# Local attention layers of a two-branch network: scores and value sums in 64x32 tiles of TensorE, values in fp32 kept in SBUF, another step order

## The chip, the cores and the metric

The kernel runs on one core of one Trainium2 chip. The metric is the device time of one execution in microseconds (us), the median over the runs. Engines are named as in the profile: PE (TensorE matmuls), PEld (its weight loads), DVE (VectorE), ACT (ScalarE), POOL (GpSimd), SP (SyncE, which issues all DMAs here).

## The reference

The input x is 2048 tokens of 128 numbers. It is normalised to xn, and two branches work on xn: a global low-rank attention of 16 heads, and a stack of six local layers. The result is x + global(xn) + local(xn). The change is in the local layers only. Cut to what matters, one of them is:

```python
def attn_layer(x, Wqkv, qs, ksc, Wo):            # x: tokens shifted by one in half of the channels
    q, k, v = split(x @ Wqkv)                    # 16 heads of 64, 128 -> 3 * 1024
    q, k = l2norm(q) * qs, l2norm(k) * ksc
    q, k = rotary(q), rotary(k)                  # with a scale per position
    # windows of 32 tokens; each sees its own and the one before: 64 keys
    sim = einsum('bhwie,bhwje->bhwij', bq, bk2) * 8.0      # masked to 32 back
    out = einsum('bhwij,bhwje->bhwie', softmax(sim), bv2)
    return out @ Wo                              # 1024 -> 128
def ffn_layer(x, g, bln, W1, b1, W2, b2):        # layernorm, 128 -> 2 * 341, a * gelu(gate), -> 128
for i in range(6):
    x = attn_layer(shift_tokens(x), ...) + x
    x = ffn_layer(shift_tokens(x), ...) + x
```

All inputs and outputs are fp32.

## The kernel before, in words

The program has two stages on the same core. The global attention comes first, with the loading of the first local weights woven in; then `LocalStack.run` does the six local layers. This stage goes over 48 steps, one for each layer L and each slice s of 256 tokens (8 slices a layer). A step consists of some 120 small pieces, each a method of `LocalStack`: `q`, `k`, `v` (projections, g from 0 to 3 for groups of four heads), `S` (scores), `sa` (mask added, out of PSUM), `mx`, `sub`, `Pr`, `ex`, `su` (softmax), `pp` and `PT` (transpose of the weights, and its eviction), `av` (value sums), `O` (divided by the sums, out of PSUM), `ot`, `oh`, `wo` (output projection), `xb` to `ffo` (feed-forward). The text `ORDER` lists all pieces with a lag, as `S.3@3`. Round n of `run` goes through this list once and does each piece for step n minus its lag, so that pieces of several steps alternate; the instructions are issued on each engine exactly in that order, and nothing reorders them (`manual_schedule`). There are 48 rounds plus the largest lag, 6.

Projections are done in split precision: the input is rounded to `xhead` with rest `xtail`, the weights to `wh` with rest `wl`, both in fp32r, and three products are added (`xh`, `xl`, `w_head`, `w_tail`; L597 for q and k, L673 for v).

Scores: a tile `kbd` of keys is block diagonal. Its 128 partitions are two heads of 64; where one head has its keys, the other has zeros. `S` (L818) does for each window of 32 tokens and each pair of heads one matmul with 128 contracted rows, 32 columns of weights (the queries) and 128 moved columns (64 keys of each of two heads), 16 for each g. They go to four 32-partition strips of one PSUM bank.

Values: `v` projects a group of heads for 256 tokens, `vc` evicts it into `vn`, `vd` stores it in DRAM, and `lv` loads it back as overlapping windows of 64 tokens into block-diagonal tiles `vbd`; `av` (L876) then does 16 matmuls of 128 rows, 32 columns of weights and 128 moved columns for each g.

PSUM has eight banks here: three of pool `pj` (projections; slots handed out by `take` and given back by `done`), two of `pT` (transposes), one for `S`, one for `av` (`pS`, `pO`), and one accumulator of `wo`.

Of the kernel before, what the change touches and what calls it, by code (L numbers as in the profile page):

```python
# [11 lines left out]
ALU = mybir.AluOpType  # L12
# [49 lines left out]
class GlobalAttention:  # L62
# [334 lines left out]
    k.0@1 wh.w1@6 ex.0@3 q1.3@2 k.1@1 tabq@1 oh.1@4 rb@2 wd.qkv.3@2 nl@5 q.0@1 O.3@4 wh.qkv.2@2 qa.0@2 lv.0.1@3 k1.0@1  # L397
    ks.1@1 sub.1@3 k2.0@1 wo.0@4 fd@6 pp.0@3 k2.1@1 wh.qkv.0@1 qa.1@2 ks.0@1 wt.w1@6 PT.0@3 ot.2@4 su.0@3 v.3@2 Pr.1@3
    qs.0@1 sa.2@3 vc.3@2 qr.1@2 k1.1@1 oh.2@4 wo.1@4 wt.qkv.2@2 ot.3@4 wd.qkv.1@1 gate@5 q1.0@1 ex.1@3 q2.0@1 wo.2@4
    oh.3@4 pp.1@3 wt.qkv.0@1 km.0@2 wh.qkv.3@2 q.2@1 mx.2@3 su.1@3 wo.3@4 fe@6 ff@6 S.3@3 xb@4 sa.3@3 av.0@3 km.1@2  # L400
    gelu@5 ka.0@1 qs.2@1 mean@4 PT.1@3 q1.2@1 v.1@1 xc@4 q2.2@1 xh@0 sub.2@3 wt.qkv.3@2 vc.1@1 O.0@3 mx.3@3 lv.1.1@3
    l0@5 km.2@2 k.2@1 vd.1@2 k.3@1 av.1@3 Pr.2@3 m0@5 ka.1@1 ww.w2@6 ks.2@1 ks.3@1 ex.2@3 k2.2@1 ha.0@1 x2@4 selk@1
    k2.3@1 kb.0@2 pp.2@3 km.3@2 qa.3@2 ot.0@3 O.1@3 sk@1 wd.qkv.0@0 k1.2@1 q.1@1 wd.w1@5 oh.0@3 k1.3@1 qs.1@1 q.3@1
    q2.1@1 ww.wo.1@4 ww.wo.0@4 qs.3@1 xl@0 qa.2@2 S.0@2 selq@1 wh.qkv.1@1 PT.2@3 var@4 q1.1@1 su.2@3 sq@1 ha.1@1
    sa.0@2 l1@5 ptn@1 sn@1 v.2@1 sub.3@3 vd.0@1 ka.3@1 Pr.3@3 lv.1.0@3 ln@4 rs@1 av.2@3 mx.0@2 wt.qkv.1@1 vc.2@1
    kb.1@2 rn@1 ex.3@3 S.1@2 ptk@1 nw@4 tabk@0 rk@1 pp.3@3 m1@5 sub.0@2 fa@5 PT.3@3 xr@4 q2.3@1 fb@5 aff@4 v.0@0 w2@5
    tk@0 O.2@3 Pr.0@2 fc@5 av.3@3 su.3@3 qr.0@1 rd@1 sa.1@2 wd.qkv.2@1 S.2@2 mx.1@2 lv.0.0@2 ot.1@3 ffo@5 vc.0@0
    ka.2@1
# [3 lines left out]
class LocalStack:  # L412
# [15 lines left out]
    def __init__(self, tc, ctx, io, const, xa, yd, out):  # L428
        self.tc, self.nc, self.io, self.c = tc, tc.nc, io, const
        self.xa, self.yd, self.out = xa, yd, out  # L430
        self.wl = {}
        self.pj = self.pT = None
        self.st = {}
        self.pw = ctx.enter_context(tc.tile_pool(name="b_w", bufs=1))
        self.pr = ctx.enter_context(tc.tile_pool(name="b_raw", bufs=1))
        self.pe = ctx.enter_context(tc.tile_pool(name="b_early", bufs=1, reuse_waits="tile"))
        self.free = {"raw": [0, 1], "pj": [0, 1, 2], "pt": [0, 1]}
        self.users = {}

    def take(self, kind, key, shape, users):  # L440

        pool = {"raw": self.pr, "pj": self.pj, "pt": self.pT}[kind]
# [16 lines left out]
    def w_whole(self, key, tag, src):  # L459
        w = self.wl[key] = self.pw.tile(list(src.shape), F32, tag=tag, name="w")  # L460
        self.nc.sync.dma_start(out=w, in_=src)
# [20 lines left out]
    def w_src(self, L, kind, i):  # L482
# [3 lines left out]
            "w1": lambda: io["w1"][L], "w2": lambda: io["w2"][L],  # L486
        }[kind]()

    def first_weights(self):
        self.vectors(0)  # L490
        for kind, i in (("wo", 0), ("wo", 1), ("w2", 0)):
# [37 lines left out]
    def buffers(self, ctx):  # L529
        nc = self.nc  # L530

# [6 lines left out]
        self.pS = pool("b_s", space=PSUM)  # L538
        self.pO = pool("b_o", space=PSUM)
# [3 lines left out]
        self.kbd = [self.pb.tile([128, 2, 2, 2, TS + 32], F32, name=f"kbd{i}") for i in range(2)]  # L543
        self.vbd = [self.pb.tile([128, 4, 2, 256], F32, name=f"vbd{i}") for i in range(3)]
        self.vn = [self.pb.tile([128, 4, 2, 2, 64], F32, name=f"vn{i}") for i in range(2)]
        for t in self.kbd:
            for j in range(2):
                nc.vector.memset(t[64 * j : 64 * j + 64, :, :, 1 - j, :], 0.0)
        for t in self.vbd:
            for j in range(2):  # L550
                nc.gpsimd.memset(t[64 * j : 64 * j + 64, :, 1 - j, :], 0.0)
        self.vturn = 0
# [114 lines left out]
    def v(self, L, s, g):  # L667
        xh, xl = self.st["xhead", L, s], self.st["xtail", L, s]
        wh, wl = self.wl["qkv", L, g]
        ps = self.take("pj", ("ps_v", L, s, g), [128, 2, 256], 1)  # L670
        for t in range(2):
            for i, (a, b) in enumerate(((xh, wh), (xh, wl), (xl, wh))):
                self.nc.tensor.matmul(ps[:, t, :], a[:, bass.ts(t, 128)], b[:, 512:768], start=(i == 0), stop=(i == 2))  # L673

    def vc(self, L, s, g):
        key = ("ps_v", L, s, g)
        self.nc.scalar.copy(
            self.vn[g // 2][:, :, g % 2], self.st[key].rearrange("p t (j q e) -> p (t j) q e", j=2, q=2)
        )
        self.done(key)  # L680

    def vd(self, L, s, gg):
        nc = self.nc
        if s == 0:
            self.st["vd", L, gg] = self.pd.tile([T + 32, 512], F32, tag=f"vd{gg}", name=f"vd{gg}_{L}")
            nc.sync.dma_start(
                out=self.st["vd", L, gg][0:32, :].rearrange("t (a e) -> t a e", a=2), in_=self.vbd[0][64:96, 0:2, 0, :]
            )
        nc.sync.dma_start(
            out=self.st["vd", L, gg][32 + s * TS : 32 + (s + 1) * TS, :].rearrange("(t p) e -> p t e", p=128),  # L690
            in_=self.vn[gg].rearrange("p (t j) g q e -> p t (j g q e)", t=2),
        )

    def lv(self, L, s, gg, i):

        vd, vbd = self.st["vd", L, gg], self.vbd[self.vturn % 3]
        self.vturn += 1
        self.st["vbd", L, s, gg, i] = vbd
        t0 = s * TS + 128 * i
        for j in range(2):  # L700
            src = vd[t0 : t0 + 64, 256 * j : 256 * j + 256]
            src = bass.AP(src.tensor, src.offset, [[512, 64], [32 * 512, 4], [1, 256]])
            self.nc.sync.dma_start(out=vbd[64 * j : 64 * j + 64, :, j, :], in_=src)
# [96 lines left out]
    def kb(self, L, s, gg):  # L800
        keys = self.st["keys", L, s, gg]
        for p in range(2):
            for j in range(2):
                for half in range(2):
                    lo, src = 64 * j + 32 * half, 32 * (2 * p + j)
                    self.nc.sync.dma_start(  # L806
                        out=self.kbd[gg][lo : lo + 32, :, p, j, :], in_=keys[src : src + 32, :, half, :]
# [3 lines left out]
    def S(self, L, s, g):  # L811
        kbd, q = self.kbd[g // 2][:, g % 2], self.st["t1q", L, s, g]
        S = self.st["S", L, s, g] = self.pS.tile([128, 8, 64], F32, tag="S", name="S")
        for i in range(2):
            for p in range(2):
                for w in range(4):
                    W = 4 * i + w
                    self.nc.tensor.matmul(  # L818
                        S[32 * w : 32 * w + 32, 4 * i + 2 * p : 4 * i + 2 * p + 2, :],
                        q[:, p, 32 * W : 32 * W + 32],  # L820
                        kbd[:, p, :, 32 * W : 32 * W + 64],
                        start=True, stop=True,
                    )

    def sa(self, L, s, g):
        S, P, mask = self.st["S", L, s, g], self.tile(("P", L, s, g), [128, 8, 64], 2), self.c["mask"]
        for i in range(2):
            if s == 0 or i == 0:
                h = slice(4 * i, 4 * i + 4 if s == 0 else 8)
                m = bmid(mask[:, i if s == 0 else 1, :], h.stop - h.start)  # L830
                self.nc.vector.tensor_tensor(P[:, h, :], S[:, h, :], m, ALU.add)
# [429 lines left out]
```

## Time and profile before

| | |
|---|---|
| median of 3 runs | 2295.75 us (2295.43 to 2300.25) |
| the profiled execution, its own time | 2285.88 us |
| its span, first to last instruction | 2284.0 us |
| mean granted PE clock in it | 0.987 of full |
| instructions | 69814, of them 27556 PE matmuls and as many weight loads |
| DMA packets, bytes | 295074, 382.40 MB |

A line of the profile for a group of instructions gives line, engine and operation, result<-operands, shapes (partitions x elements; for a matmul rows\*columns of the array, then partitions x moved columns), the count, busy time and the mean of one. An fp32 matmul stands in the trace as two records, one for each pass; an fp32r matmul as one. In a line of the stretches, each engine's busy time has its count of instructions behind it; then come the granted PE clock, the DMA engines' share and GB/s. In a line of the order of time, start and length come first; the length of a matmul has its pipeline in it, so that the start of the next block tells what one costs.

### The profile page before, as it was taken

Reading aid. Unit: us, or ns where it says so; the run is one execution under the profiler, and the core shown is the slowest. Engines: PE = TensorE matmul, PEld = TensorE weight load, DVE = VectorE, ACT = ScalarE, POOL = GpSimd, SP = SyncE. Lnnn points to the kernel's source line nnn. Section 1 sums busy time; section 2 is a strip of 40 time slices with the busy share of each in tenths; the row PEclk is TensorE's granted clock in tenths of the full one; section 3 lists DMA queues with packets and bytes.
Section 4 is the critical chain, followed back from the end, with each engine's and each line's share of the span. In section 5 each row is a group of like instructions: output and inputs, shape, how many; then the busy total and the mean of one; then the engine's idle time right before and its main releaser. Section 6 shows DMA issues by size and latency. Waiting matters only on the chain.

```text
span 2284.0 us, 69814 instructions
## 1 busy us (share of the span) xinstructions
PE 2191.6 (96%) x27556; PEld 1612.5 (71%) x27556; DVE 1880.7 (82%) x2981; ACT 1755.8 (77%) x3389; POOL 1395.3 (61%) x1417
## 2 busy tenths in 40 slices
PE   8999999999997899999999999999999999998987
PEld 3444444444445788888888888888888888887765
DVE  7999999999985687888888888788888888887764
ACT  6999999999985576777777777777777777776654
POOL 4000100000006887988898889888898888888662
PEclk9999999999999999999999999999999999999998
DMA  3223232222214788878888878888888888787662
GB/s 106 54 66 81 60 73 65 56 60 57 64 37 145 210 219 212 226 222 231 217 237 218 225 218 225 229 233 222 219 224 225 224 225 230 216 228 202 180 188 71
DMA packets 295074, 382.40 MB, mean 167 GB/s; under 512 B 38300, under 2 KB 228508, under 8 KB 293276
## 3 DMA queue, kind: packets, MB, share of 16 engines
q1 hardware_dynamic: 294732, 377.92, 61.7%
q8 instruction: 220, 3.60, 0.7%
q14 instruction: 106, 0.87, 0.1%
q10 hardware_dynamic: 16, 0.00, 0.0%
HBM read 195.06 MB, written 75.50 MB: 118 GB/s over the span
## 4 chain that ended last, share of the span: by engine, by line
PE 76%; DMA 7%; POOL 5%; SPq 4%; DVE 3%; ACT 3%; issue 2%; POOLq 0%; DVEq 0%; ACTq 0%
PE y L285 11%; PE st L275 9%; PE s L251 7%; PE ps_wo L904 5%; PE ps_o L876 5%; PE S L818 5%; PE ps_q L597 5%; PE ps_k L597 5%; PE ps_v L673 3%; PE pt_p L854 3%; PE ps_n L710 3%; PE pt_o L892 3%; SPq L806 2%; PE ps_w L1019 2%; PE ps_h L972 2%
## 5 line engine op out<-in xcount | busy, mean ns | idle before, releaser
L254 DVE TENSOR_REDUCE m<-s 128x1 f32<-128x1024 f32 x512 | 602.8, 1219 | 31.1 <-PE s L251 20.9
L277 ACT ACTIVATE p<-st 128x512 f32<-128x512 f32 x1024 | 542.4, 598 | 41.1 <-PE st L275 11.0
L305 POOL TENSOR_TENSOR z<-z 72x512 f32<-72x512 f32 x15 | 19.2, 1279 | 559.3 <-DMA z<-yp 559.3
L285 PE MATMUL y<-p,zv 128*9 128x256 f32 x4096 | 293.1, 381 | 2.3 <-ACT ysb L295 2.3
L798 POOL TENSOR_TENSOR keys<-keys,rbt 128x512 f32<-128x512 f32 x192 | 244.7, 1285 | 78.4 <-DMA rbt<-rd 75.8
L251 PE MATMUL s<-ks,qs 64*128 64x512 f32 x1024 | 280.9, 447 | 1.7 <-ACT ks L156 1.7
L275 PE MATMUL st<-qs,ks 64*128 64x512 f32 x1024 | 272.8, 433 | 1.0 <-ACT p L277 0.8
L654 POOL TENSOR_TENSOR t1q<-t1q,ur 128x512 f32<-128x512 f32 x192 | 246.7, 1286 | 24.9 <-DMA ur<-t2q 16.5
L624 POOL TENSOR_TENSOR keys<-keys,t2k 128x512 f32<-128x512 f32 x192 | 246.7, 1285 | 11.8 <-DVE keys L613 5.7
L876 PE MATMUL ps_o<-vbd,PTt 128*32 128x128 f32 x6144 | 209.0, 277 | 9.0 <-DMA vbd<-vd 7.4
L275 PEld LDWEIGHTS st<-qs,ks 64*128 64x128 f32 x1024 | 139.7, 184 | 108.1 <-ACT p L277 88.8
L818 PE MATMUL S<-kbd,t1q 128*32 128x128 f32 x6144 | 212.4, 280 | 3.0 <-DMA kbd<-keys 3.0
L838 POOL TENSOR_TENSOR P<-P,m 128x512 f32<-128x512 f32 x192 | 200.6, 1045 | 11.9 <-DVE m L834 7.3
L842 POOL TENSOR_TENSOR P<-P,r 128x512 f32<-128x512 f32 x192 | 200.6, 1045 | 0.5
L904 PE MATMUL ps_wo<-OT,w 128*128 128x256 f32 x768 | 197.1, 379 | 0.0
L876 PEld LDWEIGHTS ps_o<-vbd,PTt 128*32 128x32 f32 x6144 | 161.6, 110 | 38.4 <-ACT nh L959 13.9
L251 PEld LDWEIGHTS s<-ks,qs 64*128 64x128 f32 x1024 | 120.8, 185 | 95.0 <-issue 86.0
L818 PEld LDWEIGHTS S<-kbd,t1q 128*32 128x32 f32 x6144 | 169.0, 112 | 25.7 <-issue 16.9
L628 DVE SCALAR_TENSOR_TENSOR t1q<-ps_q,vec,tabq 128x512 f32<-128x512 f32 x192 | 143.2, 746 | 48.1 <-PE S L818 25.2
L285 PEld LDWEIGHTS y<-p,zv 128*9 128x9 f32 x4096 | 74.4, 89 | 149.0 <-issue 96.2
L658 ACT ACTIVATE sq<-ps_k 128x512 f32<-128x512 f32 x192 | 114.3, 598 | 82.6 <-PE ps_k L597 74.3
L638 DVE SCALAR_TENSOR_TENSOR t2q<-ps_q,vec,tabq 128x512 f32<-128x512 f32 x192 | 142.5, 742 | 40.5 <-ACT sq L658 38.8
(204 smaller groups left out, 5743.5 us busy)
## 6 DMA issues: line engine op xcount, KB each, us to landing
vbd<-vd SPq DMA_DIRECT2D x384, 256.0 KB
kbd<-keys SPq DMA_DIRECT2D x768, 72.0 KB
vd<-vn SPq DMA_DIRECT2D x96, 512.0 KB
ur<-t2q SPq DMA_DIRECT2D x384, 128.0 KB
rbt<-rd SPq DMA_DIRECT2D x192, 128.0 KB
tabk<-in_rope SPq DMA_DIRECT2D x48, 384.0 KB
yp<-ysb SPq DMA_DIRECT2D x64, 256.0 KB
tabq<-in_rope SPq DMA_DIRECT2D x48, 256.0 KB
```

The lines of the kernel that those rows point to most:

```text
L251: nc.tensor.matmul(s[:, j, :], q[:, bass.ts(qt, 128)], k[:, bass.ts(2 * hf + j, 512)], start=True, stop=True)
L254: nc.vector.tensor_reduce(self.mrow[h, qt // 4][:, qt % 4, hf : hf + 1], s.rearrange("p a b -> p (a b)"), AX.X, ALU.max)
L275: nc.tensor.matmul(st, k[:, bass.ts(kb, 128)], q[:, bass.ts(qb, 512)], start=True, stop=True)
L277: nc.scalar.activation(p, st, AF.Exp, scale=float(1.0 / 8.0**0.5))
L285: self.nc.tensor.matmul(self.y[32 * c : 32 * c + 9, cols], self.zv[:, kb, h, :], self.pts[h, qb, kb][:, cols], start=(j == 0 and half == 0 ...
L597: self.nc.tensor.matmul(ps[:, p, :], a[:, c], b, start=(i == 0), stop=(i == 2))
L624: self.nc.gpsimd.tensor_tensor(t, t, self.st["t2k", L, s, g], ALU.add)
L654: self.nc.gpsimd.tensor_tensor(t, t, self.st["ur", L, s, g // 2][:, g % 2], ALU.add)
L798: self.nc.gpsimd.tensor_tensor(t, t, bmid(self.st["rbt", L, s][:, g, :], 2), ALU.mult)
L818: self.nc.tensor.matmul(S[32 * w : 32 * w + 32, 4 * i + 2 * p : 4 * i + 2 * p + 2, :], q[:, p, 32 * W : 32 * W + 32], kbd[:, p, :, 32 * W ...
L876: self.nc.tensor.matmul(ps[32 * w : 32 * w + 32, i, p, :, :], PT[:, i, p, 32 * w : 32 * w + 32], vbd[:, w, :, c : c + 64], start=True, sto ...
L904: self.nc.tensor.matmul(self.st["acc", L, s], w[:, 2 * (g % 2) + c, :], o[:, c, :], start=(g == 0 and c == 0), stop=(g == 3 and c == 1),)
```

## The change

- Scores: `kbd` has no zeros and holds each head's keys in its own 64 partitions. `S` does a matmul for each head: 64 rows, 32 columns of weights, 64 moved columns; 32 for each g instead of 16. The two heads of a pair write to two banks.
- Value sums: `av` likewise, 32 matmuls of 64 rows and 32 columns, 64 moved columns.
- Values: `v` multiplies 64 tokens of the unsplit input `xa` by unsplit fp32 weights `wv` for all 16 heads, in two matmuls of 64 weight columns and 512 moved columns; `vc` evicts them to the odd windows of `vw`; `vx` builds the even (overlapping) windows with copies between partitions of SBUF by DMA. `vn`, `vd`, `lv` and `vbd` go, and the values' DRAM round trip with them; the split weights `wqkv` shrink from 768 to 512 columns a group.
- PSUM: `S` and `av` share one slot of two banks ("so"), taken by the one or the other, and given back by `sa` and by `O`.
- The list `ORDER` is another one; the largest lag is 4. Its start, and the places around `S` and `av`:

```
    av.2@3 wt.qkv.1@1 sub.0@2 q2.2@1 q1.3@1 v.0@1 O.2@3 q2.3@1 v.1@1 xh@0 rs@1 tabk@0 wd.qkv.2@1 rn@1 Pr.0@2 kb.1@2
    ...
    ks.2@0 k.3@0 su.3@2 wo.0@2 ks.3@0 selk@0 S.0@1 ww.wo.1@3 wh.qkv.0@0 PT.2@2 sk@0 k2.2@0 q.2@0 k2.3@0 PT.3@2 x2@3
    k1.2@0 ha.1@0 q.3@0 qa.2@1 qa.3@1 sa.0@1 qs.2@0 wt.qkv.0@0 qs.3@0 wd.qkv.1@0 ot.1@2 k1.3@0 S.1@1 vx@1 wh.qkv.1@0
    ka.2@0 su.2@2 selq@0 q1.2@0 mx.0@1 oh.1@2 var@3 sq@0 ptn@0 sa.1@1 sn@0
```

On PE the eight blocks of a round then stand so: av.2, v.0, v.1, av.3, v.2, (k), v.3, S.3, (wo, gate), av.0, (l0), S.2, (wo, l1, q, w2), av.1, (k, mean, wo, norm sums), S.0, (q, ot), S.1, (norm sums, variance).

```diff
-        self.free = {"raw": [0, 1], "pj": [0, 1, 2], "pt": [0, 1]}
+        self.free = {"raw": [0, 1], "pj": [0, 1, 2], "pt": [0, 1], "so": [0]}
...
-        self.kbd = [self.pb.tile([128, 2, 2, 2, TS + 32], F32, name=f"kbd{i}") for i in range(2)]
-        self.vbd = [self.pb.tile([128, 4, 2, 256], F32, name=f"vbd{i}") for i in range(3)]
-        self.vn = [self.pb.tile([128, 4, 2, 2, 64], F32, name=f"vn{i}") for i in range(2)]
+        self.kbd = [self.pb.tile([128, 2, 2, TS + 32], F32, name=f"kbd{i}") for i in range(2)]
...
-        ps = self.take("pj", ("ps_v", L, s, g), [128, 2, 256], 1)
-        for t in range(2):
-            for i, (a, b) in enumerate(((xh, wh), (xh, wl), (xl, wh))):
-                self.nc.tensor.matmul(ps[:, t, :], a[:, bass.ts(t, 128)], b[:, 512:768], start=(i == 0), stop=(i == 2))
+        ps = self.take("pj", ("ps_v", L, s, w), [128, 512], 1)
+        t0 = s * TS + 64 * w
+        for j in range(2):
+            self.nc.tensor.matmul(ps[64 * j : 64 * j + 64, :], self.xa[:, t0 : t0 + 64], wv[:, j, :], start=True, stop=True)
...
+    def vx(self, L, s):
+        nc, vw = self.nc, self.st["vw", L, s]
+        for j in range(2):
+            a, z = slice(64 * j, 64 * j + 32), slice(64 * j + 32, 64 * j + 64)
+            nc.sync.dma_start(out=vw[z, 0:8:2, :], in_=vw[a, 1:8:2, :])
+            nc.sync.dma_start(out=vw[a, 2:8:2, :], in_=vw[z, 1:7:2, :])
+            if s == 0:
+                nc.gpsimd.memset(vw[a, 0, :], 0.0)
+            else:
+                nc.sync.dma_start(out=vw[a, 0, :], in_=self.st["vw", L, s - 1][z, 7, :])
...
-        S = self.st["S", L, s, g] = self.pS.tile([128, 8, 64], F32, tag="S", name="S")
-        for i in range(2):
-            for p in range(2):
-                for w in range(4):
-                    W = 4 * i + w
+        S = self.take("so", ("S", L, s, g), [128, 2, 512], 1)
+        for b in range(4):
+            i, p = divmod(b, 2)
+            for w in range(4):
+                W = 4 * i + w
+                for j in range(2):
+                    r = slice(64 * j, 64 * j + 64)
                     self.nc.tensor.matmul(
-                        S[32 * w : 32 * w + 32, 4 * i + 2 * p : 4 * i + 2 * p + 2, :],
-                        q[:, p, 32 * W : 32 * W + 32],
-                        kbd[:, p, :, 32 * W : 32 * W + 64],
-                        start=True, stop=True,
+                        S[32 * w : 32 * w + 32, j, bass.ts(b, 64)],
+                        q[r, p, 32 * W : 32 * W + 32], kbd[r, p, 32 * W : 32 * W + 64], start=True, stop=True,
                     )
...
-        ps = self.st["ps_o", L, s, g] = self.pO.tile([128, 2, 2, 2, 64], F32, tag="o", name="ps_o")
+        ps, vw = self.take("so", ("ps_o", L, s, g), [128, 2, 512], 1), self.st["vw", L, s]
...
-                        ps[32 * w : 32 * w + 32, i, p, :, :], PT[:, i, p, 32 * w : 32 * w + 32], vbd[:, w, :, c : c + 64],
+                        ps[32 * w : 32 * w + 32, j, bass.ts(b, 64)],
+                        PT[r, i, p, 32 * w : 32 * w + 32], vw[r, 4 * i + w, c : c + 64], start=True, stop=True,
```

## The prediction

> **What bounds the kernel now.** I read the page first, then the busy time by stretches, then the order of time on PE in one period, then two small stretches of it.
>
> ```profile
> span 2284.0 us, 69814 instructions
> ...
> PE 2191.6 (96%) x27556; PEld 1612.5 (71%) x27556; DVE 1880.7 (82%) x2981; ACT 1755.8 (77%) x3389; POOL 1395.3 (61%) x1417
> ...
> PE 76%; DMA 7%; POOL 5%; SPq 4%; DVE 3%; ACT 3%; issue 2%; POOLq 0%; DVEq 0%; ACTq 0%
> ```
>
> PE leads in busy time and in the chain. The local layers run from about 696 us to the end; by stretches:
>
> ```profile
> core 0: us, PE busy (x) PEld busy (x) DVE busy (x) ACT busy (x) POOL busy (x), PEclk, DMA share, GB/s
> 696.00:900.00 204.00, 177.90 (x2417) 150.86 (x2417) 143.87 (x261) 122.64 (x244) 157.96 (x166) 0.95 0.73 200
> 900.00:2065.00 1165.00, 1151.53 (x16492) 1013.37 (x16491) 961.19 (x1814) 885.36 (x1696) 1036.35 (x1044) 1.00 0.83 225
> 2065.00:2284.00 219.00, 181.92 (x2309) 151.45 (x2307) 135.43 (x266) 119.82 (x225) 128.66 (x134) 0.93 0.58 156
> ```
>
> In the middle stretch PE is busy 98.8% of the time at full clock; POOL 89%, DVE 83%, ACT 76%, DMA 83%. The norm's variance matmul (L936) comes back every 30.8 us: that is the period of one step, and PE's own work fills it. At the two ends PE idles 26 + 37 = 63 us. So in the middle a PE microsecond saved is a microsecond gained, until the next engine is full. POOL's twelve key and query instructions follow each other every 1.245 us, its eight score instructions every 1.0 us; with the small ones that is 26.3 us a period, the floor under any gain.
>
> What PE pays for the blocks that change:
>
> ```profile
> 1405.91 1.03 PE L904 MATMUL ps_wo<-OT,w 128*128 128x256 f32 x4
> 1406.87 1.08 PE L818 MATMUL S<-kbd,t1q 128*32 128x128 f32 x32
> 1407.77 1.06 PE L876 MATMUL ps_o<-vbd,PTt 128*32 128x128 f32 x32
> 1408.75 0.70 PE L924 MATMUL ps_m<-xbt,centre 128*128 128x256 f32 x2
> 1409.10 0.47 PE L673 MATMUL ps_v<-wh,xhead 128*128 128x256 f32 x1
> 1409.41 0.28 PE L673 MATMUL ps_v<-wl,xhead 128*128 128x256 f32 x1
> ```
>
> Read starts, not lengths: a score block (16 fp32 matmuls, two passes each, 32 records) costs 0.90 us, a value-sum block the same. Inside one:
>
> ```profile
> 1406.86:1406.90 0.04, 0.03 (x4) 1.00 1.41 384
> 1406.90:1406.98 0.08, 0.08 (x4) 1.00 1.22 294
> 1406.98:1407.02 0.04, 0.04 (x7) 1.00 1.27 256
> ```
>
> Four passes start within 0.03 us (7 ns apart in the trace), then nothing starts until the next four, 0.109 us after the first: the four 32-column tiles stream 128 columns side by side. On the full array a pass of L904 takes 0.215 us for 256 columns, 0.84 ns a column; 128 columns are 0.107 us, so the stream alone sets the 0.109. Eight such waves make the block.
>
> **The change, part by part** (sum made against the profiled execution: span 2284.0, own time 2285.9; the median of the runs is 9.9 above it).
>
> *Score and value-sum blocks, 8 a period.* The head pair no longer shares one 128-row contraction with half its columns zero: 32 matmuls of 64 rows, 32 columns wide, 64 moved columns; 64 passes instead of 32. Eight tiles at 64 columns would stream 54 ns a wave, and eight starts at 7 ns take 56 ns; eight waves are 0.45, with the first weight load 0.47 us. No row shows eight tiles. Nearest rows: the four-tile block, 0.897; and the 64-row matmuls of the global attention:
>
> ```profile
> 501.21 0.50 PE L275 MATMUL st<-qs,ks 64*128 64x512 f32 x2
> 501.55 0.40 PE L251 MATMUL s<-ks,qs 64*128 64x512 f32 x2
> 501.88 0.62 PE L285 MATMUL y<-p,zv 128*9 128x256 f32 x8
> ```
>
> Each x2 is an upper-half and a lower-half matmul 3 ns apart; two pairs take 0.67 us up to the next block, so the halves do run together. Bounds: 0.45 (eight side by side) to 0.87 (four at a time: 16 waves of 54 ns) or 1.75 (one pass per 27 ns, the fastest lasting rate shown). I take 0.47, since rows and columns each overlap in this trace: 8 x (0.47 - 0.897) = -3.42 us a period.
>
> The row on issue is the 7 ns above. "TensorE: Matmul & The Clock Gate" in the Trainium skill, Part 1 ("Wait — 56ns, not 53.3ns?"), speaks against the change: start to start never falls below about 25 ns however few columns. By that a block would take 64 x 25 = 1.6 us and the kernel would end near 2630. The trace's 7 ns contradicts it only for bursts of four; no row has more.
>
> *Changes of array shape.* L904 to L818 takes 0.958 us where L904 to the next full-array block takes 0.863: +0.095 going in, and the first wave +0.025. Coming out, L818 to L924 is 0.987 against 0.897 to another 32-column block: +0.09, and L924's first pass is 0.104 longer (an uncovered 128-column weight load). One excursion costs 0.31. Before, five a period (scores, value sums, norm sums and the small transpose lie together). In the new order there are seven, and seven changes inside them (to 128x32 norm sums, to 128x64 values) at 0.115: 2 x 0.31 + 7 x 0.115 = +1.43. Between 0.6 (inner ones free) and 2.2.
>
> *Values.* Before, 4 blocks of six fp32r passes: 0.80 us each up to the next fp32 block. After, per 64 tokens two fp32 matmuls of 512 columns in 64-column tiles, two passes: 2 x 0.43 = 0.86 if the two tiles run together, as four do. +0.24; if not, +3.7.
>
> *One shared pair of banks.* Scores and value sums had a buffer each; now one slot serves both, eight uses in turn, each freed by VectorE (mask add 0.59, scaling 0.68). A waiting block holds up everything behind it on PE. The tightest place is S.0, S.1, then av.2. After S.0 ends VectorE must do mask add, k1, su, q1, mx, mask add: 0.59 + 0.68 + 0.88 + 0.75 + 0.68 + 0.59 = 4.17 by their rows. PE needs for q.2 and q.3, ot, S.1, the norm sums, the variance and a transpose 1.5 + 0.36 + 0.57 + 0.87 + 0.43 + 0.36 = 4.1: a tie. At the other seven places PE has 2 to 6 us and VectorE one or two instructions more than the freeing one. I take +0.3; bounds 0 and 1.5.
>
> *Copies and DMA.* The DRAM round trip goes: 8 loads (256 KB, 0.65 us of SP each) and 2 stores against 6 copies in SBUF, 1 MB. SP, at 87%, loses some 2.6 us a period; the copies stand after S.1 with the next key loads behind them, and wait only for value evictions half a period old. First use is 9 us of PE work later. DMA share falls from 0.83 to near 0.6. Nothing: PE was hardly waiting on these (7.4 us in all on vbd). If that cover went, 2 us a period. VectorE and ScalarE do the same elements; POOL clears two strips a layer.
>
> *Sum a period:* -3.42 + 1.43 + 0.24 + 0.3 = -1.45, so 29.35 us, still above POOL's 26.3. Times 48 steps: -70.
>
> *Order and weights.* The last lag falls from 6 to 4, 54 rounds to 52. The 63 us of PE idle at the ends belong to six rounds of lag; a third of them is -21 (bounds 0 and two periods, -59). Weight tails shrink from 768 to 512 columns, 1.84 to 1.24 us, 20 of them, 12 us of POOL; a quarter on the path, -3.
>
> Total -94: profiled 2192, median about 2202.
>
> **Rivals.**
> *Only four tiles at a time.* PE keeps four matmuls in flight, whatever their rows. For: no wave here has more than four starts. Against: the paired 64-row matmuls. A block stays at 0.87: -0.2 + 1.43 + 0.24 + 0.3 = +1.75 a period, +84 - 24: median 2356, slower. It decides where a block exceeds 0.71 us (then 8 x 0.19 plus the ends' 0.5 a period only pay the rest).
> *The shared slot eats it.* VectorE at 83% cannot free the slot in time; +1.5 us instead of 0.3 and 2.2 for shapes: net +0.5, +25 - 24: about 2297, no change. For: the tie at av.2. Against: VectorE has 5 us idle a period.
> *More than forecast.* Inner shape changes are free and nothing waits for the slot: -3.42 + 0.6 + 0.24 = -2.6 a period, 28.2, which leaves POOL at 93%: -124, with ends of -40: median 2132. For: most rows of changes going in are only 0.095. Against: every change in the trace costs something.
> The change does what it says: the built program has 39460 matmul passes against 27556, 48 x 256 more in the blocks and 48 x 8 fewer in the values.
>
> **How the numbers follow.** Forecast 2202, 0.70, its own range 2150 to 2275 (a block 0.45 to 0.55, shapes 0.6 to 2.2, ends 0 to -59). Four at a time (or slower issue) 0.16, slot 0.08, more than forecast 0.06. The range runs from 2150 to 2340: it leaves out the last of these, more than half of the first rival with the slower issue bounds, and the forecast's outer ends, some 0.2 together. About 0.2%, 5 us, is what a measurement here can tell from nothing: faster 0.76 (forecast, more than forecast), same 0.04, slower 0.20 (first rival, half of the second).
>
> **What would show it.** Right: x64 blocks of 64*32 that reach the next block in 0.45 to 0.6 us; the variance matmul every 29 to 29.7 us; PE still above 96% busy in the middle. Wrong: blocks of 0.8 us or more; waits of S or ps_o on VectorE's P or Ot over 0.5 us a period; value blocks of 1.7 us.

## The result: slower by half a per cent

The changed kernel takes 2310.42 us in the median (2303.78 to 2315.08), the kernel before 2297.44 beside it (2295.43 to 2300.25): a ratio of 1.0054, with an interval of 1.0039 to 1.0070. The forecast was 2202 and faster. The profiled execution took 2308.0 us, with a span of 2306.2 against 2284.0: 22.2 us more, where 94 less were forecast. In the medians it is 13.0 us: the profiled execution of before lies 11.6 us under its median, that of the changed kernel 2.4. The accounts below are of these two executions, so some 9 of their 22 us are in which ones were profiled.

The page of the changed kernel; in the third line come packets, MB and share of one DMA queue, the one that carries instructions:

```profile
span 2306.2 us, 93185 instructions
...
PE 2225.6 (97%) x39460; PEld 1464.4 (63%) x39460; DVE 1903.3 (83%) x2977; ACT 1725.2 (75%) x3389; POOL 1381.9 (60%) x1423
...
q8 instruction: 312, 5.11, 1.0%
...
PE 89%; DMA 3%; DVE 2%; ACT 2%; SPq 2%; issue 2%; POOL 1%; DVEq 0%; POOLq 0%; ACTq 0%
```

PE has the 39460 passes that were foreseen, is busy 34 us longer instead of less, and its share of the chain rises from 76% to 89%: it bounds the kernel more than before. Instructions come in 312 pieces of 16 KB. The page of before has this line for them:

```profile
q8 instruction: 220, 3.60, 0.7%
```

The changed kernel by stretches, the first and last of them the ends:

```profile
core 0: us, PE busy (x) PEld busy (x) DVE busy (x) ACT busy (x) POOL busy (x), PEclk, DMA share, GB/s
696.00:900.00 204.00, 184.44 (x3762) 132.59 (x3756) 146.70 (x263) 121.38 (x247) 158.62 (x166) 0.96 0.55 138
900.00:2065.00 1165.00, 1148.26 (x24928) 872.89 (x24927) 952.09 (x1756) 831.90 (x1642) 996.88 (x1021) 1.00 0.61 153
2065.00:2306.00 241.00, 213.18 (x4431) 162.20 (x4429) 166.59 (x320) 144.42 (x277) 161.19 (x166) 0.96 0.48 123
```

In the middle PE is busy 98.6% at full clock. POOL does 997 us of work there for 1036 before, since it does fewer rounds in the same time and shorter weight tails (1.29 us each for 1.83). The DMA share has fallen from 0.83 to 0.61 and brings nothing, since it was not on the path.

The order of time on PE in one round of the changed kernel; starts, not lengths, tell the prices:

```profile
1402.30 0.86 PE L796 MATMUL S<-kbd,t1q 64*32 64x64 f32 x64
1403.09 1.07 PE L686 MATMUL ps_n<-sq,sel 128*32 128x256 f32 x16
1404.09 0.70 PE L920 MATMUL ps_var<-xsq,mean 128*128 128x256 f32 x2
1404.65 0.66 PE L714 MATMUL pt_n<-ident,ssq 128*128 128x128 f32 x4
1405.23 0.98 PE L858 MATMUL ps_o<-vw,PTt 64*32 64x64 f32 x64
1406.15 1.94 PE L660 MATMUL ps_v<-w,xa 128*64 128x512 f32 x8
...
1412.76 0.95 PE L796 MATMUL S<-kbd,t1q 64*32 64x64 f32 x64
1413.64 0.66 PE L876 MATMUL pt_o<-ident,Ot 128*128 128x128 f32 x4
```

The score block S.1 reaches the next block in 0.79 us, S.3 in 0.88. Over 36 rounds, six of the eight blocks take 0.787 to 0.789 in the median, and S.0 and S.3, which have waits for their keys' DMAs between their passes, 0.881. They take 0.881 also where these DMAs had landed more than 1 us before; in S.3 above, the waves break at the 18th and 19th pass, which carry two of the waits. The forecast had 0.47 for all. Inside the block of S.1 the trace gives the starts: eight in 0.046 us, the next eights from 0.080, 0.135 and 0.191, the 32nd pass at 0.238. So the eight tiles do run side by side, a wave in some 55 ns, as foreseen. Then the waves end. Pass 33 starts at 0.266, pass 34 at 0.322, and from there they come 5 to 17 ns apart; the 64th starts at 0.641: 0.403 us for 32 passes, 12.6 ns each.

The steady part of the kernel, 36 rounds from the 4th variance matmul to the 40th, gives the ledger of a round. "Median round" means here: for every pass the median time to the next pass, all added up.

| us a round | forecast | measured |
|---|---|---|
| the eight blocks | -3.42 | 6 x 0.788 + 2 x 0.881 - 8 x 0.897 = -0.69 |
| shapes, values, shared slot | +1.97 | +1.36: the rest of the median round, 30.84 to 31.51 |
| rounds that are longer than the median one | none | +0.26: mean less median, 0.51 before, 0.76 after |
| sum | -1.45 | +0.93: mean round 31.35 to 32.27 |

The first row compares with the forecast's 0.897 a block. Before, leaving a block cost more than that at some places; with it, the eight went from 7.60 to 6.49 us, -1.11, and the 0.42 that lie between are in the second row, where the forecast has the changes of shape.

36 rounds of +0.93 are 33.3 us. The other twelve and the ends are 11.1 us shorter, that is 22 less than twelve more such rounds would be.

Last, what PE waited for in the middle stretch of the changed kernel (us in total, times, longest us); "issue" is a wait for nothing that the profile shows:

```profile
PE S L796 <- issue: 8.4, 7, 2.6
PE ps_k L584 <- ACT vw L666: 4.1, 4, 2.5
PE ps_n L686 <- issue: 2.0, 5, 0.6
PE ps_o L858 <- issue: 1.0, 3, 0.6
PE ps_v L660 <- issue: 0.7, 1, 0.7
```

Before, no wait of PE in that stretch was put down to issue. Before S and ps_o, PE does not wait for VectorE in this list.

### The profile page after: what moved, and what is told of

It reads as the page before. It is cut to its first block, busy times and chain, and to the rows that moved or that the text cites. A ratio compares the mean times of both kernels' runs of the same rounds, so it can differ in the third digit from the quotient of the medians.

```text
span 2306.2 us, 93185 instructions
## 1 busy us (share of the span) xinstructions
PE 2225.6 (97%) x39460; PEld 1464.4 (63%) x39460; DVE 1903.3 (83%) x2977; ACT 1725.2 (75%) x3389; POOL 1381.9 (60%) x1423
## 3 DMA queue, kind: packets, MB, share of 16 engines
q8 instruction: 312, 5.11, 1.0%
## 4 chain that ended last, share of the span: by engine, by line
PE 89%; DMA 3%; DVE 2%; ACT 2%; SPq 2%; issue 2%; POOL 1%; DVEq 0%; POOLq 0%; ACTq 0%
PE y L285 11%; PE st L275 8%; PE ps_wo L888 7%; PE ps_v L660 7%; PE S L796 7%; PE s L251 7%; PE ps_k L584 6%; PE ps_o L858 6%; PE ps_q L584 6%; PE ps_n L686 4%; PE pt_o L876 4%; PE pt_p L835 4%; PE ps_w L1003 3%; PE ps_g L956 2%; PE ps_h L956 2%
## 5 line engine op out<-in xcount | busy, mean ns | idle before, releaser
L645 ACT ACTIVATE sq<-ps_q 128x512 f32<-128x512 f32 x192 | 114.9, 598 | 148.9 <-PE ps_q L584 143.5
L811 DVE TENSOR_TENSOR P<-S,mask 128x512 f32<-128x512 f32 (+1 forms) x216 | 133.8, 629 | 107.8 <-PE S L796 98.7
L796 PEld LDWEIGHTS S<-kbd,t1q 64*32 64x32 f32 x12288 | 145.7, 105 | 96.5 <-issue 34.3
L888 PE MATMUL ps_wo<-OT,w 128*128 128x256 f32 x768 | 204.1, 388 | 0.3 <-ACT OT L880 0.2
L796 PE MATMUL S<-kbd,t1q 64*32 64x64 f32 x12288 | 180.9, 225 | 19.2 <-issue 11.1
L660 PE MATMUL ps_v<-w,xa 128*64 128x512 f32 x768 | 198.0, 613 | 0.7 <-issue 0.7
L858 PE MATMUL ps_o<-vw,PTt 64*32 64x64 f32 x12288 | 168.8, 224 | 5.2 <-DVE P L811 1.8
L606 DVE TENSOR_TENSOR t2k<-ps_k,tks 128x512 f32<-128x512 f32 x192 | 129.7, 679 | 53.4 <-ACT sq L645 51.4
```

The source lines that it names most:

```text
L660: self.nc.tensor.matmul(ps[64 * j : 64 * j + 64, :], self.xa[:, t0 : t0 + 64], wv[:, j, :], start=True, stop=True)
L796: self.nc.tensor.matmul(S[32 * w : 32 * w + 32, j, bass.ts(b, 64)], q[r, p, 32 * W : 32 * W + 32], kbd[r, p, 32 * W : 32 * W + 64], start= ...
L858: self.nc.tensor.matmul(ps[32 * w : 32 * w + 32, j, bass.ts(b, 64)], PT[r, i, p, 32 * w : 32 * w + 32], vw[r, 4 * i + w, c : c + 64], star ...
L888: self.nc.tensor.matmul(self.st["acc", L, s], w[:, 2 * (g % 2) + c, :], o[:, c, :], start=(g == 0 and c == 0), stop=(g == 3 and c == 1),)
```

## Experiments

**What a block's 0.79 us is.** Two theories. Supply: PE has some 32 passes with their weight loads queued when a block begins; the rest come no faster than 12 ns apart, whatever they stream. Array: after the first burst fewer than eight tiles run at a time, and the time is streaming. Three kernels change columns and passes one without the other. Twice the columns, same passes:

```diff
-                        S[32 * w : 32 * w + 32, j, bass.ts(b, 64)],
-                        q[r, p, 32 * W : 32 * W + 32], kbd[r, p, 32 * W : 32 * W + 64], start=True, stop=True,
+                        S[32 * w : 32 * w + 32, j, bass.ts(b, 128)].rearrange("q (t e) -> q t e", t=2),
+                        q[r, p, 32 * W : 32 * W + 32], bmid(kbd[r, p, 32 * W : 32 * W + 64], 2), start=True, stop=True,
... and the same in av
```

> The changed kernel with every score and value-sum matmul given its 64 moved columns twice over (128 columns, the second copy lands in unused columns of the bank): same 64 passes, same weights, twice the streaming. Supply theory (a block of 64 passes takes 0.79 us because after some 32 passes, which start in waves of eight, the rest arrive one every 13 ns or so): eight waves of 0.109 are 0.87, so streaming is now only just the longer: block to next block 0.95 to 1.0 us, some +0.2 a block, +1.6 a period, time near 2385. Array theory (after the first burst fewer than eight tiles run side by side, and 0.79 is streaming): a block doubles to 1.4 to 1.6, +5 to +6 a period, time 2550 or more.

Measured 2386.51 us, 1.0373 of before (1.0343 to 1.0403). Order of time on PE:

```profile
1414.06 1.16 PE L858 MATMUL ps_o<-vw,PTt 64*32 64x128 f32 x64
1415.14 0.65 PE L660 MATMUL ps_v<-w,xa 128*64 128x512 f32 x2
```

A block takes 1.09 us, 0.30 more for twice the columns, not 0.79 more: eight waves of 0.109 us and a tail of 0.2. Eight passes in each 0.109 us now go on to the end of the block. Streaming did not set the 0.79, though the block is 0.09 above the range that supply had put down.

Twice the passes, same columns:

```diff
-                    self.nc.tensor.matmul(
-                        S[32 * w : 32 * w + 32, j, bass.ts(b, 64)],
-                        q[r, p, 32 * W : 32 * W + 32], kbd[r, p, 32 * W : 32 * W + 64], start=True, stop=True,
-                    )
+                    for h in range(2):
+                        self.nc.tensor.matmul(
+                            S[32 * w : 32 * w + 32, j, 64 * b + 32 * h : 64 * b + 32 * h + 32],
+                            q[r, p, 32 * W : 32 * W + 32], kbd[r, p, 32 * (W + h) : 32 * (W + h) + 32], start=True, stop=True,
+                        )
... and the same in av
```

> The changed kernel with every score and value-sum matmul cut in two of 32 columns: same columns streamed in all, 128 passes a block for 64. Supply theory: 32 passes from the queue, then 96 at 13 ns, and the tail of 0.145: 1.45 to 1.65 us a block for 0.79, some +6 a period, time near 2600. Array theory: the same streaming, so 0.79 to 0.85 and no change of the time beyond 1 per cent.

Measured 2793.54 us, 1.2142 (1.2096 to 1.2188), further above before than supply had said (near 2600). A block that is not held up, and two that are, in the order of time on PE:

```profile
1414.06 1.48 PE L797 MATMUL S<-kbd,t1q 64*32 64x32 f32 x128
1415.46 0.66 PE L878 MATMUL pt_o<-ident,Ot 128*128 128x128 f32 x4
...
1422.83 0.36 PE L860 MATMUL ps_o<-vw,PTt 64*32 64x32 f32 x18 [1.95 <-issue]
...
1426.94 0.41 PE L797 MATMUL S<-kbd,t1q 64*32 64x32 f32 x32 [0.94 <-issue]
```

The undisturbed block takes 1.40 us: 32 passes in 0.21 and 96 in 1.08, 11.2 ns each. A pass of 32 columns costs about as much as one of 64: the number of passes sets the time. The rest of the 480 us over the changed kernel is the second thing: blocks that stand still for 1 to 2 us in their midst, of which more below.

Half the passes, same columns, by merging the two pairs:

```diff
-        for b in range(4):
-            i, p = divmod(b, 2)
+        for i in range(2):
...
-                        S[32 * w : 32 * w + 32, j, bass.ts(b, 64)],
-                        q[r, p, 32 * W : 32 * W + 32], kbd[r, p, 32 * W : 32 * W + 64], start=True, stop=True,
+                        S[32 * w : 32 * w + 32, j, bass.ts(i, 128)].rearrange("q (t e) -> q t e", t=2),
+                        q[r, 0, 32 * W : 32 * W + 32], kbd[r, :, 32 * W : 32 * W + 64], start=True, stop=True,
... and the same in av
```

> The changed kernel with the two pairs of a block merged in one matmul of 128 columns: 32 passes a block for 64, same columns streamed (both pairs use the first pair's weights, so that part of the computation is changed). Supply theory: all 32 come from the queue: four waves of 0.109 and the tail of 0.145, 0.55 to 0.60 us a block for 0.79, -0.2 each, -1.6 a period, -75 at most; time 2235 to 2270, since some of it goes to waits of other engines. Array theory: the block stays at 0.79 and the time at 2310. The forecast's own price, 0.47, would need eight waves of 54 ns; this kernel streams as many columns and shows whether the waves at least reach it.

Measured 2233.49 us, 0.9706 (0.9688 to 0.9725). Order of time on PE:

```profile
1415.61 0.67 PE L795 MATMUL S<-kbd,t1q 64*32 64x128 f32 x32
1416.20 0.70 PE L886 MATMUL ps_wo<-OT,w 128*128 128x256 f32 x2
```

0.60 us: four clean waves, the last pass at 0.398, and 0.2 to the next block. With half the passes the columns of the changed kernel go through in a quarter less time, and the kernel, which gives both pairs the first pair's weights, is 66 us faster than before. This settles it for the number of passes.

Is it a queue that fills again? Five of the eight blocks cut in two, 32 passes each, with another step of PE between:

```diff
-    O.3@3 k.0@0 ... S.3@2 su.0@2 ot.2@3 ...
+    O.3@3 k.0@0 ... S.3@2 su.0@2 ot.2@3 Sz.3@2 ...
... S.0, S.2, av.0, av.1 likewise; S and av do b = 0, 1, and Sz and az do b = 2, 3
```

> The changed kernel with five of its eight blocks cut in two halves of 32 passes, the second half after the next step on PE (S.0, S.2, S.3, av.0, av.1); same instructions, other places. Supply theory with a queue of some 32 pairs filled while PE does other work: both halves run all in waves of eight, last start 0.23 to 0.25 us after the first, next block at 0.36 to 0.43; two halves 0.72 to 0.86 where the block takes 0.79, and each more excursion costs some 0.2 to 0.3: period +1 to +1.5, time 2350 to 2390. Rival, by which the burst is not refilled or 12 ns a pass holds from the start of a half whose place has a short step before it: last start at 0.35 to 0.4 and time 2380 to 2420.

Measured 2345.73 us, 1.0202 (1.0166 to 1.0239), 4 us under the range. Order of time on PE:

```profile
1400.66 0.45 PE L872 MATMUL ps_o<-vw,PTt 64*32 64x64 f32 x32
1401.04 0.66 PE L890 MATMUL pt_o<-ident,Ot 128*128 128x128 f32 x4
1401.63 0.46 PE L872 MATMUL ps_o<-vw,PTt 64*32 64x64 f32 x32
1402.01 0.66 PE L842 MATMUL pt_p<-ident,P 128*128 128x128 f32 x4
```

Every half that has no waits for key DMAs inside has its last start at 0.238 us, the second halves too, 0.6 us after the first one's end in the lines above; the next block comes at 0.384 (at 0.50 in one place, after the second half of av.1). So the 32 are there again after other work on PE. The two halves together cost as much as the block (0.77), and the five further excursions raised the median round by 1.07 us, some 0.2 each.

What lies behind the 12 ns is not told apart by these runs: fetching and decoding, or starting the weight loads. The loads as such are not serial: each is 102 to 107 ns long in the trace, and they start about 7 ns apart in the first half of a block and, in pairs, two every 16.6 ns in the second.

**The tiles alone.** Order, values and slot of the changed kernel, blocks of 128 rows:

```diff
-                for j in range(2):
-                    r = slice(64 * j, 64 * j + 64)
-                    self.nc.tensor.matmul(
-                        S[32 * w : 32 * w + 32, j, bass.ts(b, 64)],
-                        q[r, p, 32 * W : 32 * W + 32], kbd[r, p, 32 * W : 32 * W + 64], start=True, stop=True,
-                    )
+                self.nc.tensor.matmul(
+                    S[32 * w : 32 * w + 32, 0, bass.ts(b, 128)].rearrange("q (t e) -> q t e", t=2),
+                    q[:, p, 32 * W : 32 * W + 32], bmid(kbd[:, p, 32 * W : 32 * W + 64], 2), start=True, stop=True,
+                )
... and the same in av
```

> The tiles undone alone: the changed kernel's order, values and shared slot, but scores and value sums again as 16 matmuls of 128 rows by 32 columns with 128 moved columns a block, 32 passes (the two heads of a pair are summed, so that part of the computation is changed; the instructions and times are those of the old block). Supply theory: a block takes 0.90 us as before, for 0.79 (0.88 with a wait inside): +0.75 a period by the blocks alone, less what the changes of shape to 64 rows cost, so that the tiles are worth 10 to 36 us: 2320 to 2346. A rival, by which 64-row tiles cost more at their borders than they save: time 2290 to 2310, and the tiles are the part that makes the changed kernel slow. By the forecast's block (0.47 for 0.90) it would be 2440 or more.

Measured 2331.03 us, 1.0131 (1.0112 to 1.0151). Order of time on PE:

```profile
1411.50 1.06 PE L794 MATMUL S<-kbd,t1q 128*32 128x128 f32 x32
1412.48 0.38 PE L584 MATMUL ps_q<-xhead,wh 128*128 128x256 f32 x1
...
1414.53 1.08 PE L794 MATMUL S<-kbd,t1q 128*32 128x128 f32 x32
1415.43 0.40 PE L686 MATMUL ps_n<-sq,sel 128*32 128x256 f32 x4
```

A block costs 0.90 ahead of 32-column work, 0.99 to 1.01 ahead of other shapes. So the tiles are worth some 20 us, not the 164 (48 x 3.42) of the forecast, and it is the rest of the change that makes the kernel slower. One thing was not expected: the rounds here are 32.79 in the median and 32.78 in the mean, all alike, and PE has no wait on issue. With the tiles the median round is 1.28 shorter, and only 0.50 is left of that in the mean.

**The late starts.** A count from the traces shows what they are. Taken are all gaps of more than 0.6 us between starts on PE in the same 36 rounds, and of these the ones that end 1.2 to 1.7 us after a 16 KB piece of the queue q8 has landed:

| kernel | passes in all | such pieces | gaps, us | of these 1.2 to 1.7 us after a piece, us |
|---|---|---|---|---|
| before | 27556 | 220 | 18.1 | 0.0 |
| 128-row blocks | 27172 | 216 | 2.8 | 0.0 |
| half the passes | 27172 | 216 | 35.3 | 1.1 |
| changed | 39460 | 312 | 23.1 | 17.1 |
| twice the columns | 39460 | 312 | 6.2 | 5.6 |
| twice the passes | 64036 | 504 | 173.1 | 168.1 |

With a piece every 5.9 us in the changed kernel, a stretch of 0.5 us would hold one gap in twelve by chance; it holds 14 of 18. The last column follows the passes in a microsecond: 0 to 1.1 us with 27 thousand, little where as many as in the changed kernel are spread over longer blocks, 4.7 us of every round with 64 thousand. A piece of 16 KB at 5.11 MB for 78920 PE instructions is 253 instructions, two blocks' worth, and in every other kernel here it is 250 to 254. So the pieces are PE's, and PE waits here for its own program. In the changed kernel most of it falls on S.1 (median 0.79 us, mean 1.03) and the norm sums behind it (1.00 and 1.15): the end of the list ORDER, where S.1, av.2 and av.3 and the values stand close together. To test it, S.1 alone goes back to 128 rows:

```diff
+                if g == 1:
+                    self.nc.tensor.matmul(
+                        S[32 * w : 32 * w + 32, 0, bass.ts(b, 128)], q[:, p, 32 * W : 32 * W + 32],
+                        kbd[:, p, :, 32 * W : 32 * W + 64], start=True, stop=True,
+                    )
+                    continue
... kbd again with zeros in the other head's half
```

> The changed kernel with one of its eight blocks, S.1, back in 128 rows by 32 columns (its keys again with zeros in the other head's half): 32 passes for 64 in the stretch that has most passes a microsecond (S.1, norm sums, variance, value sums, values). Theory of the fetch: there instructions run out because they are used faster than pieces of them arrive; with 32 pairs fewer the late starts go: S.1 from a mean of 1.03 us to 0.90, the norm sums from 1.15 to 0.98 (same shape as S.1 now), the waits on nothing before S and norm sums from 10 us to under 4 in the middle stretch; -0.3 to -0.45 a round, time 2288 to 2298. Rival, by which the late starts come from something else that is late by then (weights, another engine): S.1 0.90, but the lateness turns up at the next blocks: 2303 to 2313.

Measured 2300.92 us, 0.9996 of before (0.9978 to 1.0014): no difference from before, where the changed kernel is 0.54% slower. Waits of PE in the middle stretch, only the first two of them:

```profile
PE ps_k L586 <- ACT vw L668: 4.7, 5, 1.8
PE S L804 <- issue: 2.2, 5, 1.1
```

S.1 takes 0.897 us in the mean, the norm sums 0.998, and the gaps that follow a piece fall from 17.1 us to 2.0. The median round is unchanged (31.51), the mean falls from 32.27 to 31.88. A block that is 0.11 us longer by itself makes the round 0.40 shorter, since 32 passes are gone from the crowded stretch. These two traces overstate the gain: the execution profiled here lies 8.8 us under its median, and in the medians the gain is 9.5 us, 0.2 a round. The time is 3 us above the range, so the sign and the mechanism hold and the size nearly does.

**Other values, for the rest of the loss.** In the changed kernel the four value blocks take 3.89 us a round (1.87 for two, then 1.01 each) for 3.36 before. Three versions bring the fp32r products back, each with three matmuls of 128 tokens by 512 columns on the full array:

```diff
-        for j in range(2):
-            self.nc.tensor.matmul(ps[64 * j : 64 * j + 64, :], self.xa[:, t0 : t0 + 64], wv[:, j, :], start=True, stop=True)
+        for n, (a, b) in enumerate(((xh, wh), (xh, wl), (xl, wh))):
+            self.nc.tensor.matmul(ps, a[:, bass.ts(i, 128)], b, start=(n == 0), stop=(n == 2))
...
-        self.nc.scalar.copy(self.st["vw", L, s][:, 2 * w + 1, :], self.st[key])
+        for h in range(2):
+            self.nc.scalar.copy(
+                self.st["vw", L, s][64 * j : 64 * j + 64, 4 * i + 2 * h + 1, :], self.st[key][64 * h : 64 * h + 64, :]
+            )
```

> The changed kernel with its values as before, three fp32r products on the full array (128 tokens by 512 columns each, the weights split into head and tail again), evicted straight into the two tokens halves of the SBUF buffer by two copies of 64 partitions; everything else as changed. Theory: the value blocks cost what they cost because fp32 needs two passes of 512 columns in two tiles, and because the array changes shape for them: from 3.9 us a period for four blocks to about 2.5, cadence 31.4 to 29.9 or 30.2; ScalarE gets 2.3 us a period more, still under 28. Time 2240 to 2260, which would beat both kernels. Rival: ScalarE's longer evictions and the weight splits at each layer's border take it back: 2290 to 2310. If instruction fetch sets the pace at the blocks (the waits on nothing that I see before scores and norm sums), the gaps of 0.5 us or more that end 1.2 to 1.7 us after a fetched piece stay or grow, and the mean round stays some 0.8 above the shortest.

Measured 2374.02 us, 1.0325 (1.0302 to 1.0348): a miss. Waits of PE in the middle stretch:

```profile
PE ps_v L661 <- ACT vw L669: 28.0, 33, 0.9
PE ps_k L584 <- ACT vw L669: 19.7, 62, 1.1
```

The result has both tokens' halves in one bank, and the buffer wants each by itself on other partitions. Two copies of 64 partitions (0.58 us each) cost ScalarE twice one of 128 (0.59), the three slots of pj come free later, and PE waits 1.4 us a round for them. Without waits the value blocks take 1.49 and 0.89, so PE would gain 0.6 a round. The same with 128-row blocks:

> Tiles and values both undone, order, shared slot and copies in SBUF kept (128-row score and value-sum blocks as in the run before it, so the two heads of a pair are summed; values in three fp32r products). With the other three it makes the four corners: order alone, tiles alone, values alone, both. If the parts just add, its time is that of the run with 128-row blocks plus what the values give in the run beside this one: 2331 - (50 to 70) = 2260 to 2280, so that the order alone is worth -15 to -40 against before. Rival: the order is what costs (one slot for two tiles, more changes of shape) and it lands at 2295 to 2310, no better than before. Rounds should be as even as with the 128-row blocks, since PE takes in half as many instructions there.

Measured 2399.8 us, 1.0439 (1.0415 to 1.0464): it has the same waits (29.9 and 21.3 us), so it says nothing of the order alone. Next, one copy of 128 partitions into a staging tile, and DMAs from there:

```diff
+    def vy(self, L, s):
+        vs, vw = self.st["vs", L, s], self.tile(("vw", L, s), [128, 8, 512], 2)
+        for j in range(2):
+            for h in range(2):
+                self.nc.sync.dma_start(
+                    out=vw[64 * j : 64 * j + 64, 2 * h + 1 : 8 : 4, :], in_=vs[64 * h : 64 * h + 64, :, j, :]
+                )
```

> The changed kernel with its values in three fp32r products on the full array again, but now with one eviction of 128 partitions a block (as many ScalarE copies as the changed kernel has) into a staging tile, four more DMAs a step from there to the two halves, and the weight splits spread over the round. The run before it failed on the eviction: two copies of 64 partitions for one cost ScalarE what PE saved, and PE waited for them. Theory: PE saves 1.2 to 1.6 us a period on the value blocks, the waits on vw go, cadence 29.9 to 30.2, time 2240 to 2265. Rival: the four DMAs on SP (at 16 KB or more a piece and 1 MB a period) delay keys or queries behind them, or POOL's two more weight splits delay the norm factors: 2280 to 2310. What the fetch of instructions costs should stay, some 0.4 to 0.8 us a round above the shortest.

> The same with the 128-row score and value-sum blocks (two heads of a pair summed): both tiles and values undone, the order, the shared slot and the copies in SBUF kept: the corner that the other run with two evictions missed. If the parts add: the time with 128-row blocks (2331) less what the values give in the run beside it (45 to 70): 2261 to 2286, and the order alone is worth -15 to -40 against before. Rival: 2295 to 2310: the order gives nothing, and its shared slot and changes of shape eat the gain at the ends.

Measured 2498.72 us (1.0863, 1.0837 to 1.0889) and, with 128-row blocks, 2441.87 (1.0610, 1.0587 to 1.0633), both far above all that was expected. The chain that ended last, and PE's longest wait in the middle stretch, of the first of them:

```profile
PE 53%; DMA 12%; DVE 8%; POOL 8%; SPq 7%; ACT 6%; issue 5%; POOLq 0%; DVEq 0%; ACTq 0%
...
PE pt_p L844 <- ACT P L836: 41.5, 41, 6.2
```

The waits on vw are gone, and PE's share of the chain falls from 89% to 53% while DMA and SP's queue go from 5% to 19%. That would fit four more DMAs in SP's queue delaying all others behind them, but it is not shown: which of them is the first to be late was not traced. Last, one of the two copies on VectorE:

```diff
+        for h, copy in enumerate((self.nc.scalar.copy, self.nc.vector.tensor_copy)):
+            copy(self.st["vw", L, s][64 * j : 64 * j + 64, 4 * i + 2 * h + 1, :], self.st[key][64 * h : 64 * h + 64, :])
```

> The changed kernel with values in three fp32r products on the full array; of the two half evictions one goes to ScalarE, one to VectorE, no DMA is added. From the first try of the kind: its value blocks without their waits took 1.49 and 0.89 us where the changed kernel's take 1.87 and 1.01, so PE saves 0.62 a period, not the 1.2 to 1.6 that I had put down. Theory: with ScalarE's share back at four copies, PE no longer waits on the evictions: -0.62 x 48 = -30, time 2275 to 2290. Rival: VectorE, at 82 per cent with four copies more (2.4 us a period), frees the shared slot later, and ScalarE's copies of 64 partitions are no shorter: 2300 to 2330.

> The two before it together. If both theories hold they add: -45 to -50 against the changed kernel, time 2258 to 2270, which would beat both kernels. If only one holds, the time of that one; if VectorE is the bound, 2295 to 2330.

Measured 2416.8 us (1.0501, 1.0474 to 1.0528), and 2406.57 (1.0461, 1.0434 to 1.0489) with S.1 in 128 rows as well, both again above all that was expected. Waits of PE in the middle stretch of the first:

```profile
PE ps_k L584 <- DVE vw L669: 48.6, 34, 3.0
PE pt_p L838 <- ACT P L830: 15.0, 4, 4.2
PE ps_o L861 <- DVE P L814: 13.6, 32, 0.8
PE ps_v L661 <- DVE vw L669: 13.4, 33, 0.4
```

The rival named the right engine, but most of the time goes another way than it said: PE waits for VectorE's copies of the values, which hold slots of pj, 1.9 us a round, and for the mask addition that frees the shared slot 0.4. So values on the full array cost more outside PE than they save on it, in three ways of moving them. No version here that does the whole computation beats the kernel before; the best (S.1 in 128 rows) only equals it. What the order alone is worth stays open.

## Why the prediction was wrong, step by step

- *The blocks* are the step that failed. The text took 0.47 "since rows and columns each overlap in this trace", and both do: waves of eight at 55 ns. But the price of eight waves was worked out from the array alone. The rate at which passes can be had was read off bursts of four, 7 ns, though the same text said that "no row has more". It is 7 ns for 32 passes and 11 to 12.6 after that. 0.81 in the mean for 0.47 is 2.73 us a round, 131 us in 48 rounds, more than the whole miss of 116 (-94 to +22 in the profiled executions; between the medians it is 108).
- The skill's table of theoretical speedup ("TensorEngine Tiling (Array Packing)", Overview) gives up to twice for a contraction of 64. The waves show it, 55 ns for 109; the whole block shows 0.897 / 0.788 = 1.14 and 0.897 / 0.881 = 1.02.
- The bounds, 0.45 to 1.75, held the value. The text then took the low end, by the row nearest in shape (the paired 64-row matmuls), not the row nearest in number of passes, of which there was none.
- *The first rival* was right in its point of decision and wrong in its mechanism. It said that above 0.71 us a block the change loses; blocks took 0.79 and 0.88, and it lost. With 0.81 its sum gives -0.69 + 1.97 = +1.28 a round, +61 - 24, a median near 2333. Not four tiles at a time, but 32 passes at full rate and a slower supply after them.
- The skill's rule that was weighed, at least 25 ns from start to start ("TensorE: Matmul & The Clock Gate", Part 1), gives by estimate 64 x 25 ns = 1.6 us a block. Counted over all tiles of the array the runs show 7 ns, then 11 to 12.6. The rule pointed the right way and the row the wrong one; the value lies between.
- *Shapes, values, slot*: forecast +1.97, measured +1.36, 29 us too much in 48 rounds. The values gave +0.52 with their shape changes. The shared slot, +0.3, cost nothing that the trace shows: in the median VectorE's freeing instruction ended 0.73 to 4.5 us before each of the eight blocks began, 0.96 before av.2, where the text had a tie.
- *Late starts by instruction fetch*: in no term and no rival, +0.26 a round net, some 12 us in these two executions. The gaps after a piece alone are 17.1 / 36 = 0.47 a round; the other gaps fell from 18.1 us to 6.0. The page of before had the row of q8, and 43% more passes were in the text.
- *Ends and weights*: forecast -21 and -3, measured -22 together, all of it behind the 40th variance matmul. The number is right; that the lag is its cause was not tested. PE's idle time in the first and last stretch together fell from 63 to 47 us.
- *Copies and DMA*: forecast nothing, and nothing is what came of the lower DMA share.

With 2 us for the ends, 131 - 29 + 12 + 2 is 116, the distance between -94 and +22. The range, 2150 to 2340, held the result; the likeliest case's own, up to 2275, did not.

## What to carry to other kernels

Price a block of small matmuls by two numbers and take the larger: columns streamed in waves, and passes that have to be supplied, with a first lot (32 here) that is queued and the rest at a steady rate (11 to 13 ns here). Halving the work of a matmul by doubling the number of them stops paying when a pass streams for less than that rate times the tiles that run at once (here 12.6 ns x 8 = 0.10 us, and a pass of 64 columns streams in 0.055); doubling also makes the program longer (220 pieces to 312 here), and it has to be fetched. Before trusting a burst rate from a trace, look for the longest burst that it has, and if the new block is longer, keep the range that its length leaves open and put the likeliest value inside it.

## What the hardware showed that was not expected

- Eight 64x32 tiles run side by side: 8 starts in 46 ns, waves of 55 ns for 64 columns and 0.109 us for 128, up to 32 passes; then 11.2 ns a pass (32 columns) or 12.6 (64).
- After 0.6 us of other work on PE the first 32 passes of a block are fast again (0.238 us both times).
- PE can run out of instructions: 17.1 us in 36 rounds of the changed kernel, 168.1 with twice the passes, in gaps that end 1.2 to 1.7 us after a 16 KB piece of its program has landed; 0 to 1.1 us with 27 thousand passes in the kernel.
- Waits for DMAs that have landed long before still cost time inside a block: 0.881 us for 0.788.
- One more excursion to 64x32 tiles and back costs about 0.2 us a round (1.07 for five).
